# Adjacency products of a GRU layer from an fp32r high part and the rest: two one-pass matmuls in place of one two-pass fp32 matmul

## The chip, the cores and the metric

One core of a Trainium2 chip runs the whole program. The metric is the time of one execution in device microseconds (us), the median of several. Every experimental kernel was timed in three rounds beside the kernel before, on the same chip. The experiments ran in five batches on five chips, where before took 6768 to 6788 us (medians), so kernels of different batches are best compared by their ratios to before.

## The reference

64 graphs of 256 nodes with 256 features pass through three attention layers and one GRU layer. Every layer starts with a layer norm and a relu, and adds its result to x. The change is in the GRU layer. Cut to what matters:

```python
# layers 0, 1, 2: graph attention: softmax over neighbours, then attention @ features
# layer 3:
h = relu(layernorm(x))
A = (adj != 0).astype(float32)
for i in range(3):
    aggr = einsum('bst,bsd->btd', A, h @ weight[i])   # A is 0 or 1
    h = gru_cell(aggr, h, w_ih, w_hh, b_ih, b_hh)
return x + h
```

## The kernel before

Two graphs (a pair, 512 nodes) are worked on at a time, so there are 32 pairs. While TensorE does the attention layers of one pair, the GRU work of the pair before it is put between them. Each of the three GRU steps has a block of adjacency products ("block 1, 2, 3"), which read node features `hn` by rows and the adjacency `am`. All of it is fp32:

```python
def norm_t(xt, want_rows=False):
    ...                                            # layer norm to xn, transposed to ht
    hn = work.tile([P, C, D], F32, name="hn")
    nc.gpsimd.tensor_scalar(hn, xn, 0.0, None, op0=OP.max)          # L203
    return ht, hn
...
for h in range(H):                                 # layer 1, four heads
    for t in range(T):                             # five edge types
        nc.tensor.matmul(                          # L335: HT = 20 rows only
            ps, lhsT=ident[:HT, r : r + 1].to_broadcast([HT, P]), rhs=ed, ...)
...
for i in range(L):                                 # the GRU's three steps
    for dc in range(DC):
        for b in range(2):
            for sc in range(2):
                nc.tensor.matmul(                  # L415: a block is 8 of these
                    ps[:, b * N : (b + 1) * N],
                    lhsT=hn[:, 2 * b + sc, dc * P : (dc + 1) * P],
                    rhs=am[:, 2 * b + sc, :], start=(sc == 0), stop=(sc == 1))
        nc.scalar.copy(ag[:, dc, :], ps)
    ...                                            # gate products (L431), activations
    for b in range(2):                             # the new state, transposed to rows (L469)
        ...
        elif b == 0:
            nc.vector.tensor_copy(dst, ps)         # L480
        else:
            nc.scalar.copy(dst, ps)
```

## Time and profile before

| | before |
|---|---|
| time, median of 3 (range) | 6774.84 us (6770.32 to 6777.54) |
| TensorE busy | 5559.1 us, 82% of the span |
| VectorE (DVE), ScalarE (ACT), GpSimd (POOL) busy | 54%, 41%, 22% |
| mean granted TensorE clock | 0.829 |
| period of one pair (mean of 30) | 206.15 us |
| of it at half clock | 67.5 us |

TensorE is the bound: in most of a pair it works without a gap. But its granted clock is 1.00 or 0.50, never anything else (full and half clock below; "warm" is full clock), and in a third of the pair, 67.5 of 206.15 us, it is 0.50. A product of L431 follows the one before it after 0.43 us at full clock and 0.85 us at half, and "busy" counts that longer time.

Every stretch at one clock, but for the one that the end of the trace cuts off, is a whole multiple of 3.413 us long (at half clock mostly 3.41, 6.83 or 10.24 us), and all changes of the clock lie on one grid of that step, to within 0.01 us. One such step is called a window here. In before a half-clock stretch of 3.41 us starts at 3013.40, 1.06 us behind B's idle of 2.42 us, and one of 10.24 us starts at 3047.53, among eight 20-row products (L335), with TensorE 100% busy on both sides of the change (windows 3043.00:3047.53 and 3047.54:3057.77).

For all kernels I cut the pair into nine stretches at the same instructions: S1 (block 1 to the scores of layer 0's last head), A (to that head's first transpose, a wait for its softmax), S2 (to layer 0's last attention product), B (to the first transpose of layer 1's norm, a wait), S3 (layer 1, the long one), C (to the norm of layer 2, a wait), S4, D (the softmax of layer 2, a wait), S5.

### The profile page before, as it was taken

How to read it: one execution, taken by the hardware profiler on the slowest of the kernel's cores; microseconds unless marked ns; L12 is line 12 of the kernel's file. 1: busy time of each engine (PE TensorE's matmuls, PEld its weight loads, DVE VectorE, ACT ScalarE, POOL GpSimd, SP SyncE). 2: the span in 40 equal slices, each digit the busy share in tenths (PEclk: the TensorE clock that was granted, in tenths of full speed). 3: DMA queues.
4: the chain of work that ended last, by engine and by line, in shares of the span. 5: the costliest groups of instructions: out<-in, count | busy, mean ns of one | idle time of the engine just before them, and what ended most of it. 6: DMA issues, size and time to landing. Idle time of an engine off the chain costs nothing.

```text
span 6767.9 us, 53845 instructions
## 1 busy us (share of the span) xinstructions
PE 5559.1 (82%) x18480; PEld 3152.6 (47%) x18480; DVE 3627.6 (54%) x5756; ACT 2765.8 (41%) x6925; POOL 1512.0 (22%) x967
## 2 busy tenths in 40 slices
PE   5688988888978889888889788788878897888887
PEld 3444544444544445444445444445444454444453
DVE  4555555555555555555555555555555555555553
ACT  2344443344433444434444334444334443344442
POOL 1222122221122221222211222212222112222111
PEclk7788888888888878888788888888888888887888
DMA  1000000000000000000000000000000000000000
GB/s 54 0 10 10 4 10 7 10 10 10 4 7 10 10 10 4 10 7 10 10 10 4 7 10 10 10 10 4 7 10 10 10 4 7 10 10 7 4 1 6
DMA packets 55361, 59.15 MB, mean 9 GB/s; under 512 B 3120, under 2 KB 54192, under 8 KB 55088
## 3 DMA queue, kind: packets, MB, share of 16 engines
q1 hardware_dynamic: 54080, 53.88, 2.7%
q8 instruction: 146, 2.39, 0.2%
q10 hardware_dynamic: 1008, 1.84, 0.1%
q14 instruction: 127, 1.04, 0.1%
HBM read 38.93 MB, written 16.78 MB: 8 GB/s over the span
## 4 chain that ended last, share of the span: by engine, by line
PE 70%; DVE 16%; POOL 10%; ACT 2%; issue 1%; DMA 0%; DVEq 0%; POOLq 0%; SPq 0%; ACTq 0%
PE bank_psb L431 29%; PE bank_psa L335 11%; PE bank_psa L260 8%; PE bank_psa L245 5%; PE bank_psb L415 5%; PE bank_psa L211 4%; PE bank_psa L222 3%; DVE st L181 2%; DVE u L230 2%; DVE nm L232 2%; PE bank_psa L196 2%; POOL rstd L185 2%; POOL var L367 1%; POOL hn L203 1%; POOL en L305 1%; ACT u L235 1%
## 5 line engine op out<-in xcount | busy, mean ns | idle before, releaser
L431 PE MATMUL bank_psb<-ag,wc 128*128 128x512 f32 x2304 | 1263.5, 667 | 0.0
L431 PE MATMUL bank_psb<-ht,whh 128*128 128x512 f32 x2304 | 1217.6, 647 | 0.0
L457 POOL TENSOR_TENSOR d<-ht,n 128x512 f32<-128x512 f32 x192 | 254.6, 1326 | 3774.4 <-ACT n L451 3774.4
L342 ACT ACTIVATE e<-bank_psa,wh 128x256 f32<-128x256 f32 x2560 | 981.0, 478 | 282.8 <-PE bank_psa L335 270.9
L346 DVE COPY_PREDICATED u<-masks,e 128x1024 f32<-128x1024 uint8 x640 | 832.7, 1301 | 361.7 <-ACT e L342 359.7
L335 PE MATMUL bank_psa<-ed,ident 20*128 20x512 f32 x1280 | 775.0, 744 | 0.7 <-ACT ed L326 0.7
L235 ACT ACTIVATE u<-u,nm 128x256 f32<-128x256 f32 x1152 | 570.2, 497 | 429.3 <-DVE nm L232 420.5
L196 PE MATMUL bank_psa<-ident,xn 128*128 128x128 f32 x1024 | 202.8, 346 | 659.3 <-DVE xn L188 639.7
L431 PEld LDWEIGHTS bank_psb<-ag,wc 128*128 128x128 f32 x2304 | 477.5, 216 | 562.1 <-issue 547.5
L260 PEld LDWEIGHTS bank_psa<-wh,pt 128*128 128x128 f32 x4608 | 647.4, 205 | 146.5 <-issue 79.8
L431 PEld LDWEIGHTS bank_psb<-ht,whh 128*128 128x128 f32 x2304 | 439.7, 202 | 580.6 <-issue 566.6
L260 PE MATMUL bank_psa<-wh,pt 128*128 128x64 f32 (+1 forms) x4608 | 691.1, 302 | 0.1
L245 PE MATMUL bank_psa<-ident,u 128*128 128x128 f32 x2304 | 443.8, 313 | 264.8 <-ACT u L235 264.4
L245 PEld LDWEIGHTS bank_psa<-ident,u 128*128 128x128 f32 x2304 | 310.8, 158 | 568.0 <-ACT u L235 499.7
L199 ACT ACTIVATE ht<-bank_psa 128x512 f32<-128x512 f32 x256 | 146.0, 596 | 847.0 <-PE bank_psa L196 840.6
L196 PEld LDWEIGHTS bank_psa<-ident,xn 128*128 128x128 f32 x1024 | 148.7, 168 | 726.2 <-issue 596.1
L415 PE MATMUL bank_psb<-am,hn 128*128 128x256 f32 x1536 | 452.2, 447 | 7.5 <-POOL hn L203 2.6
L335 PEld LDWEIGHTS bank_psa<-ed,ident 20*128 20x128 f32 x1280 | 256.4, 215 | 333.3 <-issue 259.3
L415 PEld LDWEIGHTS bank_psb<-am,hn 128*128 128x128 f32 x1536 | 332.3, 228 | 115.0 <-issue 33.2
L269 DVE TENSOR_TENSOR o<-bank_psa,rs 128x256 f32<-128x256 f32 x256 | 108.7, 425 | 497.0 <-PE bank_psa L260 491.2
L469 PE MATMUL bank_psb<-ident,ht 128*128 128x128 f32 x768 | 166.8, 345 | 239.6 <-DVE ht L459 239.6
L455 ACT ACTIVATE z<-bank_psb,bg 128x512 f32<-128x512 f32 x192 | 131.8, 687 | 566.9 <-PE bank_psb L431 566.9
(89 smaller groups left out, 6671.2 us busy)
## 6 DMA issues: line engine op xcount, KB each, us to landing
xt<-in_x_dram SPq DMA_DIRECT2D x32, 512.0 KB, 4.9
at<-in_adj_dram SPq DMA_DIRECT2D x32, 512.0 KB, 3.8
out_dram<-hn SPq DMA_DIRECT2D x32, 512.0 KB, 3.2
whh<-in_L_gnn_w_hh_dram SPq DMA_DIRECT2D x1, 768.0 KB, 8.8
w<-in_L_gnn_weight_dram SPq DMA_DIRECT2D x3, 256.0 KB, 4.4
wih<-in_L_gnn_w_ih_dram SPq DMA_DIRECT2D x1, 768.0 KB, 6.6
a1b<-in_L_gnn_a_src_dram ACTq DMA_DIRECT2D x1, 640.0 KB, 7.2
a1b<-in_L_gnn_a_dst_dram ACTq DMA_DIRECT2D x1, 640.0 KB, 9.7
```

The costliest lines, as they stand in the source:

```text
L196: nc.tensor.transpose(ps[:, c * P : (c + 1) * P], xn[:, c, dc * P : (dc + 1) * P], ident)
L211: nc.tensor.matmul(ps[:, :m], lhsT=ht[:, dc, c * P : (c + 1) * P], rhs=we[:, dc, :m], start=(dc == 0), stop=(dc == DC - 1),)
L222: nc.tensor.matmul(ps, lhsT=wd[:, dc, h : h + 1].to_broadcast([P, P]), rhs=ht[:, dc, :], start=(dc == 0), stop=(dc == DC - 1),)
L235: nc.scalar.activation(u[:, c, :], u[:, c, :], AF.Exp, bias=nm[:, c : c + 1], accum_out=sm[:, c : c + 1])
L245: nc.tensor.transpose(ps[:, jc * N + ic * P : jc * N + (ic + 1) * P], u[:, 2 * b + ic, jc * P : (jc + 1) * P], ident,)
L260: nc.tensor.matmul(ps, lhsT=pt[:, b, jc, ic * P : (ic + 1) * P], rhs=wh[:, 2 * b + jc, f0:f1], start=(jc == 0), stop=(jc == 1),)
L335: nc.tensor.matmul(ps, lhsT=ident[:HT, r : r + 1].to_broadcast([HT, P]), rhs=ed, start=True, stop=True,)
L342: nc.scalar.activation(e[:, c, :], ps[:, b * N : (b + 1) * N], AF.Identity, bias=wh[:, c, D + r : D + r + 1],)
L346: nc.vector.copy_predicated(u, masks[:, t], e)
L415: nc.tensor.matmul(ps[:, b * N : (b + 1) * N], lhsT=hn[:, 2 * b + sc, dc * P : (dc + 1) * P], rhs=am[:, 2 * b + sc, :], start=(sc == 0), s ...
L431: nc.tensor.matmul(ps, lhsT=w[:, dc, g * P : (g + 1) * P], rhs=v[:, dc, :], start=(k == 0), stop=(k == n - 1),)
L457: nc.gpsimd.tensor_tensor(d, ht[:, j, :], n, op=OP.subtract)
```

## The change

The products of the blocks are to become cheaper. Before, each is two hardware matmuls ("two-pass" below: 768 in the source, 1536 in the profile, 0.22 us each at full clock). The adjacency is 0 or 1. An fp32 feature is split into a high part, written as fp32r, and the rest. Each part then takes one hardware matmul ("one-pass": still 1536 matmuls, for twice as many products), and both parts are summed in the same fp32 tile `ps` (`start` and `stop` in the diff). The order of TensorE's instructions is left to the scheduler, so it changes too. Docstrings and comments also went.

```diff
-        hn = work.tile([P, C, D], F32, name="hn")
-        nc.gpsimd.tensor_scalar(hn, xn, 0.0, None, op0=OP.max)
+        hn = work.tile([P, 2, C, D], F32R, name="hn")
+        nc.gpsimd.tensor_scalar(hn[:, 0], xn, 0.0, None, op0=OP.max)
+        nc.vector.scalar_tensor_tensor(
+            hn[:, 1], xn, 0.0, hn[:, 0].bitcast(F32), op0=OP.max, op1=OP.subtract
+        )
@@ gru
-        am = work.tile([P, C, N], F32, name="am", bufs=1)
+        am = work.tile([P, C, N], F32R, name="am", bufs=1)
@@
-                        nc.tensor.matmul(
-                            ps[:, b * N : (b + 1) * N],
-                            lhsT=hn[:, 2 * b + sc, dc * P : (dc + 1) * P],
-                            rhs=am[:, 2 * b + sc, :],
-                            start=(sc == 0), stop=(sc == 1),
-                        )
+                        for part in range(2):
+                            nc.tensor.matmul(
+                                ps[:, b * N : (b + 1) * N],
+                                lhsT=hn[:, part, 2 * b + sc, dc * P : (dc + 1) * P],
+                                rhs=am[:, 2 * b + sc, :],
+                                start=(sc + part == 0), stop=(sc + part == 2),
+                            )
@@
-            hn = work.tile([P, C, D], F32, name="hn")
+            if last:
+                res = work.tile([P, C, D], F32, name="res", bufs=1)
+            else:
+                hn = work.tile([P, 2, C, D], F32R, name="hn")
@@
-                elif b == 0:
-                    nc.vector.tensor_copy(dst, ps)
                 else:
-                    nc.scalar.copy(dst, ps)
+                    nc.scalar.copy(pair(hn[:, 0]), ps)
+                    nc.vector.tensor_sub(pair(hn[:, 1]), ps, pair(hn[:, 0]).bitcast(F32))
```

More of the change, by code (lines that the diff above doesn't have):

```diff
@@ L9 @@
 F32 = mybir.dt.float32
+F32R = mybir.dt.float32r
 I32 = mybir.dt.int32
@@ L473, in gru, with pair @@
                         )
-                dst = hn[:, 2 * b : 2 * b + 2, :].rearrange("p c d -> p (c d)")
+                def pair(t):
+                    return t[:, 2 * b : 2 * b + 2, :].rearrange("p c d -> p (c d)")
                 if last:
-                    nc.vector.tensor_add(
-                        dst, xt[:, 2 * b : 2 * b + 2, :].rearrange("p c d -> p (c d)"), ps
-                    )
-                elif b == 0:
-                    nc.vector.tensor_copy(dst, ps)
-                else:
-                    nc.scalar.copy(dst, ps)
+                    nc.vector.tensor_add(pair(res), pair(xt), ps)
+                else:
+                    nc.scalar.copy(pair(hn[:, 0]), ps)
+                    nc.vector.tensor_sub(pair(hn[:, 1]), ps, pair(hn[:, 0]).bitcast(F32))
             yield
-        nc.sync.dma_start(out_v[:, p * C : (p + 1) * C, :], hn)
+        nc.sync.dma_start(out_v[:, p * C : (p + 1) * C, :], res)
         yield
```

## The prediction

> **What bounds the kernel now.** I read the page first (busy shares, chain, groups), then the timeline of TensorE over one pair of graphs, then windows with the granted clock.
>
> ```profile
> span 6767.9 us, 53845 instructions
> ...
> PE 5559.1 (82%) x18480; PEld 3152.6 (47%) x18480; DVE 3627.6 (54%) x5756; ACT 2765.8 (41%) x6925; POOL 1512.0 (22%) x967
> ...
> PE 70%; DVE 16%; POOL 10%; ACT 2%; issue 1%; DMA 0%; DVEq 0%; POOLq 0%; SPq 0%; ACTq 0%
> ...
> L415 PE MATMUL bank_psb<-am,hn 128*128 128x256 f32 x1536 | 452.2, 447 | 7.5 <-POOL hn L203 2.6 <-DVE hn L480 0.9
> ```
>
> TensorE is the bound, but not everywhere: 70% of the chain that ended last is its own work, 26% is DVE and POOL work for which it stands idle. The products that the change touches (L415) take 452 of 5559 us. Each source matmul is two hardware ones here (768 in the source, 1536 in the row).
>
> The timeline of TensorE shows the period of one pair, 206.1 us on average (first L415 of pair 1 at 279.2 us, of pair 31 at 6463.7, 30 periods). It has four stretches in which TensorE waits for a chain of other engines, whatever else it has to do: A, the softmax of layer 0's last head; B, the layer norm after layer 0; C, the norms after layer 1; D, the softmax of layer 2. B looks so:
>
> ```profile
> 3000.69 1.00 PE L260 MATMUL bank_psa<-wh,pt 128*128 128x64 f32 x8
> 3001.53 3.24 PE L415 MATMUL bank_psb<-am,hn 128*128 128x256 f32 x14
> 3004.60 1.88 PE L431 MATMUL bank_psb<-ht,whh 128*128 128x512 f32 x4
> 3006.32 1.88 PE L431 MATMUL bank_psb<-ag,wc 128*128 128x512 f32 x4
> 3008.04 1.88 PE L431 MATMUL bank_psb<-ht,whh 128*128 128x512 f32 x4
> 3012.34 2.04 PE L196 MATMUL bank_psa<-ident,xn 128*128 128x128 f32 x8 [2.42 <-DVE xn L188]
> ```
>
> The last attention product of layer 0 (L260) ends at 3001.53; the norm that follows from it reaches TensorE at 3012.34, 10.8 us later. In between lie 14 of the 16 L415 matmuls, and TensorE idles 2.42 us at the end. This is a wait for DVE, so a shorter L415 only lengthens the idle. Starts divided by counts: an L415 matmul takes 0.22 us (3.07/14), an L431 0.43 us (1.72/4).
>
> The windows show the clock:
>
> ```profile
> core 0: us, PE busy (x) PEld busy (x) DVE busy (x) ACT busy (x) POOL busy (x), PEclk, DMA share, GB/s
> 3050.50:3057.00 6.50, 6.50 (x8) 2.08 (x7) 3.85 (x3) 3.02 (x8) 0.00 (x0) 0.50 0.00 0
> 3071.50:3074.80 3.30, 3.30 (x10) 2.55 (x9) 2.60 (x2) 3.30 (x9) 0.00 (x0) 0.50 0.00 0
> 3076.40:3083.30 6.90, 6.90 (x17) 3.08 (x17) 5.38 (x5) 3.66 (x9) 0.00 (x0) 1.00 0.34 76
> 2958.30:3163.90 205.60, 171.22 (x577) 96.09 (x577) 112.62 (x179) 86.14 (x216) 47.24 (x30) 0.84 0.03 8
> ```
>
> TensorE runs at half or full clock, and can be at 0.50 while 100% busy. Over one pair the mean is 0.84, so about a third of the time is at half speed. The half-speed stretches follow the L335 matmuls, which have 20 rows only, and the idle times.
>
> [...]
>
> **The change, part by part.**
> Removed: 1536 two-pass L415 matmuls of 0.22 us, warm. Added: 1536 one-pass ones (768 x 2 parts). I take each at 0.11 us[...]. That is 16 x 0.11 = 1.76 us less in each of the three blocks of a pair, warm. In the third block, which lies partly at half clock (its matmuls take 5.8 to 6.5 us), up to about 3 less. Were all of it on the path: 32 x (1.76 + 1.76 + 3) = 209 us, 3.1%. That is the ceiling.
>
> Added on DVE: per pair one 128x1024 subtract (1.22 us, as L230) and four 128x512 from PSUM (0.68) against two copies (0.67): +2.6 us; ACT two more copies of 0.58. Neither is near full, so this counts as latency only. After the transposes TensorE must now wait for an ACT copy and then a DVE subtract, where two copies ran beside each other.
>
> Order matters more. The compiled orders of both kernels have the same 72 gate products (0.86 us each, two matmuls) per pair, but the scheduler spreads them differently. Before, 12 lie inside the waits A, B, C, where they are free or nearly so (4, 6 and 2; one more, after B's wait, is alike in both). After, 7 (2, 5, 0). So 5 gate products move onto TensorE-bound stretches: 2 between D and A, 3 between B and C.
>
> Block 1 (after layer 3's norm):
>
> ```profile
> 3161.03 2.78 POOL L203 TENSOR_SCALAR hn<-xn 128x1024 f32<-128x1024 f32 x1 [1.58 <-DVE xn L188]
> 3163.82 1.66 DVE L294 SCALAR_TENSOR_TENSOR u<-bank_psa,wh,cap 128x256 f32<-128x256 f32 x4 [2.96 <-PE bank_psa L222]
> 3163.86 3.72 PE L415 MATMUL bank_psb<-am,hn 128*128 128x256 f32 x16
> ```
>
> POOL's hn is ready at 3163.81, just as L415 starts. The low part needs one more DVE pass of 1.22 us, so TensorE stalls some 1.2 us of the 1.76 saved: 0.6 is won. The pass also stands ahead of L294, which starts 1.25 us later; the two gate products moved forward cover that. This stretch: -0.6 + 2 x 0.86 = +1.1 us.
> Up to the end of layer 0's last attention product: one L415 and five transposes moved behind it: -1.0 us.
> Block 2: inside B: 0. Its idle grows to about 2.9 us.
> Block 3 (layer 1, TensorE-bound): the transposes come late, behind the softmax; the second half's high part is copied by ACT only after four exponentials. I estimate 2 us of stalls, of which before shows half already. Net of that -2.7 us with its half clock, plus three gate products at mixed clock, +2.6 to +3.1: about +0.2 us.
> Sum: +0.3 us a pair.
>
> Clock: idle before A's end grows from 1.31 to about 3 us (3.4 of gate products became 1.7). B's 2.42 us made a half-speed window of 3.41 us; A's 1.31 did not. So A may now do so, which costs up to 1.7 us. In block 3's half-speed window there is now half the L421 work beside two 20-row matmuls, so a second such window is likely in some pairs. I put +0.8 us on both. Total +1.1 us a pair, x 32 = +35 us: 6775 + 35 = 6810 us.
>
> **The rivals.**
> First, "the saving goes through": TensorE is 82% busy, so 209 us less work gives 3% less, 6570 us. For it: the 70% of the chain. Against it: block 2 is inside a wait, block 1 loses most to the new DVE pass, and freed time in A to C is not refilled.
> Second, "the clock takes it": more idle and thinner work mean more half-speed windows; two more a pair cost 3.4 us, 32 x 3.4 = 109 us, 6880 to 6920 us. For it: periods before come as 204.8, 205.6 and 207.4 us, in step with 3.41 us windows, so small shifts may jump by a window.
> Third, "the new chain binds": copy then subtract in the ACT and DVE queues delays transposes and softmax of the next head, +2 us a pair, 6840 to 6870 us. For it: the queue order at block 3. Against it: ACT 41% and DVE 54% busy.
> Fourth, one-pass matmuls that do not run at 0.11 us (weight loads not overlapped): at 0.2 us nothing is saved, and the time is near 6900 us.
>
> **Range and chances.** The first rival is damped by the arithmetic above, and half of it (3 us a pair) gives 6680. The second and third together give 6930. So 6810, range 6700 to 6930. Faster by over 2% (below 6639) needs nearly all the ceiling on the path, 0.08; slower by over 2% (above 6910) needs two extra half-speed windows or slow one-pass matmuls, 0.12; the rest 0.80.
>
> **What will show it.** In the changed profile the L421 group should have 1536 matmuls, about 0.11 us apart when warm, and TensorE's busy time should fall by 150 to 230 us at a span that hardly moves. The idle at L197 for DVE xn, and at L250 for ACT u, should grow; new idle should stand at L421 for DVE hn (1.2 us in block 1, more in block 2). DVE should write hn 160 times (five a pair). The clock should be at or a little below 0.83. I am wrong if the period drops below 203 us: then the moved gate products or block 3's stalls cost less than I take them for, or half-speed windows vanish.

## The result, and the profile after

The kernel after takes 6932.65 us (median of 4, 6931.14 to 6933.39) against 6776.19 us (median of 4) in the same rounds: ratio 1.0234, interval 1.0220 to 1.0249, **slower by over 2%**. A ratio here is the mean time of one kernel's fast runs over that of the other's of the same rounds, so not quite the ratio of the medians quoted. The prediction was 6810 us, with 6700 to 6930 as its range; the measured time lies just outside. All outputs are right.

The page of the kernel after (span; busy time by engine; the chain that ended last; the group of the changed products, with busy time, mean ns of one, and idle time before them):

```profile
span 6931.6 us, 53910 instructions
...
PE 5604.3 (81%) x18480; PEld 3201.7 (46%) x18480; DVE 3766.8 (54%) x5852; ACT 2800.4 (40%) x6989; POOL 1534.2 (22%) x967
...
PE 70%; DVE 17%; POOL 8%; ACT 2%; issue 2%; DMA 0%; DVEq 0%; SPq 0%; ACTq 0%; POOLq 0%
...
L421 PE MATMUL bank_psb<-am,hn 128*128 128x256 f32 x1536 | 364.2, 391 | 34.9 <-DVE hn L206 27.1
```

The changed products did get shorter (452.2 to 364.2 us, though many now run at half clock). TensorE's busy time nevertheless rose, from 5559.1 to 5604.3 us. No work was added on TensorE, so the time of the same instructions rose: that is the clock, 0.794 on the mean after 0.829.

The waits of TensorE (who waited for whom; us in total, times, longest), before:

```profile
PE bank_psa L196 <- DVE xn L188: 639.7, 66, 24.2
PE bank_psa L245 <- ACT u L235: 264.4, 145, 6.6
PE bank_psb L469 <- DVE ht L459: 239.6, 65, 4.6
```

and after:

```profile
PE bank_psa L197 <- DVE xn L189: 704.7, 66, 24.2
PE bank_psa L250 <- ACT u L240: 312.9, 72, 6.6
PE bank_psb L478 <- DVE ht L465: 216.8, 65, 5.4
PE bank_psb L421 <- DVE hn L206: 27.1, 31, 0.9
```

The two old waits grew by 65 and 49 us, the third shrank by 23, and the new wait at L421 is 27 us. That is 118 us in all; with the 45 us more of busy time (5559.1 to 5604.3) it makes the 163 us by which the span grew (163.7).

The timeline of TensorE after (start, length, then idle before it and its releaser), at block 1 and from stretch A to the end of B:

```profile
3031.87 0.38 PE L421 MATMUL bank_psb<-am,hn 128*128 128x256 f32 x1
3033.13 2.06 PE L421 MATMUL bank_psb<-am,hn 128*128 128x256 f32 x15 [0.88 <-DVE hn L206]
...
3069.04 0.38 PE L478 MATMUL bank_psb<-ident,ht 128*128 128x128 f32 x2
3072.93 0.45 PE L250 MATMUL bank_psa<-ident,u 128*128 128x128 f32 x1 [3.50 <-ACT u L240]
...
3079.89 3.81 PE L421 MATMUL bank_psb<-am,hn 128*128 128x256 f32 x16
...
3089.44 1.41 PE L197 MATMUL bank_psa<-ident,xn 128*128 128x128 f32 x8 [1.46 <-DVE xn L189]
```

Block 1 is as foreseen: a stall of 0.88 us, then 15 products in 1.90 us (3033.13 to 3035.03), 0.127 us each. Stretch A ends with 3.50 us of idle, and block 2 takes 3.64 us for 16 (to 3083.53), 0.23 each: it lies at half clock.

The windows after (length, then busy time and instructions of PE, PEld, DVE, ACT and POOL, then the clock):

```profile
3144.67:3154.91 10.24, 10.24 (x19) 4.43 (x18) 7.10 (x6) 7.79 (x21) 0.00 (x0) 0.50 0.17 51
3072.99:3083.23 10.24, 10.21 (x44) 8.89 (x45) 2.54 (x5) 4.21 (x11) 3.81 (x2) 0.50 0.00 0
3031.87:3243.50 211.63, 173.50 (x577) 99.09 (x577) 117.13 (x182) 87.22 (x218) 48.03 (x30) 0.80 0.03 8
```

The second line is the half-clock time that starts 0.06 us after A's idle has ended; the prediction's pair has none there. The first line lies in head 3 of layer 1, around block 3, with TensorE 100% busy: 10.24 us at half clock, where the prediction's pair has 3.41 (its line at 3071.50 shows 3.30 of them). What TensorE does there before:

```profile
3067.23 3.69 PE L335 MATMUL bank_psa<-ed,ident 20*128 20x512 f32 x8
3070.86 4.54 PE L415 MATMUL bank_psb<-am,hn 128*128 128x256 f32 x12
3075.33 1.12 PE L335 MATMUL bank_psa<-ed,ident 20*128 20x512 f32 x2
```

and after:

```profile
3142.70 5.27 PE L340 MATMUL bank_psa<-ed,ident 20*128 20x512 f32 x8
3147.89 2.07 PE L421 MATMUL bank_psb<-am,hn 128*128 128x256 f32 x8
3149.90 2.07 PE L340 MATMUL bank_psa<-ed,ident 20*128 20x512 f32 x2
```

Between two lots of products with 20 rows stood 4.5 us of products with 128 rows; now 2.0 us stand there, and half clock covers them all and runs on.

By stretch (mean of 30 pairs, worked out from the traces; us, and in brackets how much of it at half clock; e2b, e3b and e4b are experiments below):

```
        before          after           e2b             e3b             e4b
S1      32.23 (0)       33.69 (0)       34.09 (0)       33.05 (0)       33.69 (0)
A        6.90 (0)        7.37 (0.01)     7.37 (0.62)     6.90 (0)        7.37 (0)
S2       4.15 (0)        5.65 (5.58)     5.65 (5.65)     5.69 (4.17)     3.69 (0)
B       10.82 (0)       10.86 (4.65)    10.86 (3.97)    10.87 (6.07)    10.82 (0.38)
S3      98.01 (36.18)   99.91 (40.85)   93.55 (21.16)  100.32 (40.62)  101.93 (43.99)
C       25.17 (20.63)   25.70 (22.59)   25.71 (23.42)   25.17 (17.76)   25.70 (22.63)
S4+D+S5 28.87 (10.65)   28.45 (11.55)   27.91 (10.72)   29.51 (12.97)   28.42 (11.51)
pair   206.15 (67.5)   211.63 (85.2)   205.15 (65.5)   211.50 (81.6)   211.63 (78.5)
```

In B and C TensorE waits for other engines, and half clock costs next to nothing there: B takes 10.82 us with none of it, 10.86 with 4.65 us (before, after). In S2 and S3 I take it to cost half its length, as with the products of L431 (0.85 us for 0.43). That is an estimate, and for S2 a high one: e4b has 5.58 us less of it there than after, and S2 is 1.96 us shorter, not 2.8. Taking that half off gives what these stretches would take at full clock, waits included: S1 + A + S2 + S3 is 123.20 us before and 123.40 after. So that hardly changed, and (5.58 + 40.85 - 36.18) / 2 = 5.1 of the 5.48 us that a pair got longer are, by that estimate, half clock in S2 and S3.

The same can be counted over the whole pair, with TensorE's busy time (as at full clock), its idle time, and what half clock adds to the busy time (taken as half of the busy time at half clock) kept apart (us a pair, worked out from the same traces; e8 and e9 are before and after with 128 rows in place of 20):

```
              before   after    e2b      e8       e9
work          148.4    143.0    148.3    146.2    142.5
idle           34.3     38.1     37.0     36.7     40.8
half clock     23.4     30.5     19.8     11.6     11.3
pair          206.15   211.63   205.15   194.55   194.56
```

So the saving was there, 5.4 us a pair, and 3.9 us of it became idle time; half clock then took 7.0: 5.0 of them in S1 to S3, where they lengthen the pair, and 2.3 in B, which stayed at 10.8 us. (Before and e8 have the same products with the same columns and differ by 2.2 us in work, so read no difference finer than that.)

### The profile page after: what moved, and what is told of

It is laid out like the page before. It is cut to its first block, busy times and chain, and to the rows that moved or that the text cites. A ratio compares the mean times of both kernels' runs of the same rounds, so it can differ in the third digit from the quotient of the medians.

```text
span 6931.6 us, 53910 instructions
## 1 busy us (share of the span) xinstructions
PE 5604.3 (81%) x18480; PEld 3201.7 (46%) x18480; DVE 3766.8 (54%) x5852; ACT 2800.4 (40%) x6989; POOL 1534.2 (22%) x967
## 4 chain that ended last, share of the span: by engine, by line
PE 70%; DVE 17%; POOL 8%; ACT 2%; issue 2%; DMA 0%; DVEq 0%; SPq 0%; ACTq 0%; POOLq 0%
PE bank_psb L437 30%; PE bank_psa L340 12%; PE bank_psa L265 9%; PE bank_psa L250 6%; PE bank_psa L216 4%; PE bank_psa L227 3%; PE bank_psb L421 3%; DVE st L182 2%; DVE u L235 2%; POOL rstd L186 1%; POOL var L372 1%; PE bank_psa L197 1%; POOL hn L205 1%; POOL en L310 1%; DVE ht L465 1%
## 5 line engine op out<-in xcount | busy, mean ns | idle before, releaser
L437 PE MATMUL bank_psb<-ht,whh 128*128 128x512 f32 x2304 | 1326.2, 696 | 0.0
L437 PE MATMUL bank_psb<-ag,wc 128*128 128x512 f32 x2304 | 1162.2, 620 | 0.0
L340 PE MATMUL bank_psa<-ed,ident 20*128 20x512 f32 x1280 | 855.5, 816 | 0.7 <-ACT ed L331 0.7
L197 PE MATMUL bank_psa<-ident,xn 128*128 128x128 f32 x1024 | 181.2, 322 | 724.1 <-DVE xn L189 704.7
L265 PEld LDWEIGHTS bank_psa<-wh,pt 128*128 128x128 f32 x4608 | 695.7, 220 | 142.9 <-issue 65.1
L437 PEld LDWEIGHTS bank_psb<-ht,whh 128*128 128x128 f32 x2304 | 476.4, 220 | 614.3 <-issue 606.4
L265 PE MATMUL bank_psa<-wh,pt 128*128 128x64 f32 (+1 forms) x4608 | 742.0, 318 | 0.1
L250 PE MATMUL bank_psa<-ident,u 128*128 128x128 f32 x2304 | 470.2, 331 | 313.6 <-ACT u L240 312.9
L257 DVE COPY pt<-bank_psa 128x512 f32<-128x512 f32 x288 | 199.1, 691 | 400.0 <-PE bank_psa L250 400.0
L421 PE MATMUL bank_psb<-am,hn 128*128 128x256 f32 x1536 | 364.2, 391 | 34.9 <-DVE hn L206 27.1
L448 ACT ACTIVATE r<-bank_psb,bg 128x512 f32<-128x512 f32 x192 | 131.3, 684 | 607.1 <-PE bank_psb L437 607.1
L421 PEld LDWEIGHTS bank_psb<-am,hn 128*128 128x128 f32 x1536 | 297.4, 275 | 148.8 <-issue 47.7
```

Of the source, the lines that this page charges most:

```text
L197: nc.tensor.transpose(ps[:, c * P : (c + 1) * P], xn[:, c, dc * P : (dc + 1) * P], ident)
L250: nc.tensor.transpose(ps[:, jc * N + ic * P : jc * N + (ic + 1) * P], u[:, 2 * b + ic, jc * P : (jc + 1) * P], ident,)
L265: nc.tensor.matmul(ps, lhsT=pt[:, b, jc, ic * P : (ic + 1) * P], rhs=wh[:, 2 * b + jc, f0:f1], start=(jc == 0), stop=(jc == 1),)
L340: nc.tensor.matmul(ps, lhsT=ident[:HT, r : r + 1].to_broadcast([HT, P]), rhs=ed, start=True, stop=True,)
L421: nc.tensor.matmul(ps[:, b * N : (b + 1) * N], lhsT=hn[:, part, 2 * b + sc, dc * P : (dc + 1) * P], rhs=am[:, 2 * b + sc, :], start=(sc + ...
L437: nc.tensor.matmul(ps, lhsT=w[:, dc, g * P : (g + 1) * P], rhs=v[:, dc, :], start=(k == 0), stop=(k == n - 1),)
```

## The experiments

Two questions: is it the new order of TensorE's instructions or the one-pass products themselves; and is the clock the cause, or only what goes with a new chain of waits (copy, then subtract)?

### Order and operations apart

To hold an order, every matmul and transpose is recorded where it is made, and at the end each GRU instruction is tied behind and ahead of its neighbours by edges of the class NoSync. (The profiles of these kernels show the lines of the helpers, L173 to L184.)

```diff
+    for p in range(NP - 1):
+        last = None
+        for k, m in ORDER:     # which GRU instruction, how many of the attention's stand before it
+            g, m = made["gru"][p * ng + k], na * (p + 1) + m
+            if last is not None:
+                behind(g, last)
+            last = g
+            for q in made["att"][m - 8 : m]:
+                behind(g, q)
+            for q in made["att"][m : m + 8]:
+                behind(q, g)
```

The first table held only counts, not which instruction stands where, so a transpose that must wait for the GRU's state (L469) came before gate products that need not. Four runs have this flaw. e2 is the old operations in the order of after; e3 the new operations with the gate products where before has them; e4 is after with three products that nobody reads in A's idle; e7 is before with 128-row products (edit below).

> The kernel before (fp32 products, its own copies), with TensorE's instructions held in the changed kernel's order (two fewer gate products in the wait for the last softmax of layer 0, three more in layer 1). Theory 'order and clock': the idle before that softmax grows from 1.31 us to about 3 us, the half-clock window that follows in the changed kernel appears here too, and the gate products that left the waits add 4 us: 6 to 8 us a pair more, 6950 to 7020 us, clock near 0.79. Theory 'new chain' (the extra copy and subtract make the changed kernel slower, order does not matter): within 1% of 6775 us.

Measured: 6828.03 us, ratio 1.0088 [1.0071, 1.0104].

> The changed kernel, with the gate products put where the kernel before has them (four in the wait for the last softmax of layer 0, six in the wait for the norm after it, two after layer 1), all else as in the changed kernel's order. Theory 'order and clock': idle before that softmax falls from 3.5 to about 1.8 us, no half-clock stretch after it, S1 1.7 us and layer 1 2.6 us shorter: about 205 us a pair, 6700 to 6790 us, clock 0.82 or more. Theory 'new chain': stays at 6880 to 6935 us.

Measured: 6842.20 us, ratio 1.0108 [1.0093, 1.0123].

> The changed kernel in its own order, with three idle fp32 products of 128x512 (2.6 us, read by nobody) for TensorE in the wait for the last softmax of layer 0. Theory 'clock': TensorE idles 0.9 us there instead of 3.5, the 10.24 us at half clock that follow do not come, the 2.7 us that the transposes and attention products lost there come back: about 209 us a pair, 6830 to 6870 us. Theory 'the idle costs only itself': 6930 us, or more by what the filler delays.

Measured: 7032.32 us, ratio 1.0389 [1.0374, 1.0405].

> The kernel before in its own order, with the 20-row products of layer 1 (L335) made over 128 rows, the added ones zero: the same columns, so the same time at a given clock. If the clock gate looks at how much of the array works: most of layer 1's 36 us at half clock a pair vanish, up to 18 us a pair: 6250 to 6600 us, clock 0.88 or more. If it looks at something else (idle time alone, or the values, which are zero): 6775 us within 1%.

Measured: 6367.21 us, ratio 0.9407 [0.9393, 0.9421], clock 0.883.

The waits of e2 show the flaw (before, this wait came 65 times and cost 239.6 us):

```profile
PE bank_psb L178 <- DVE ht L472: 324.0, 96, 3.6
```

In e4 the filling products queued behind such a transpose and stretch A grew to 11.70 us. So e2, e3 and e4 decide nothing by themselves; in e7 the effect is far larger than the flaw. The table then named each instruction, and the runs were repeated.

> As e2, but with each transpose of the GRU's state in its own place too (e2 held only the counts, and TensorE waited for a state in the wait for the last softmax). fp32 products and the copies of before, TensorE in the changed kernel's order. Theory 'order and clock': an idle of over 3 us before that softmax, a half-clock stretch after it, S1 and layer 1 longer by the gate products that left the waits: 4 to 8 us a pair, 6900 to 7020 us, clock 0.79 to 0.80. Theory 'new chain': within 1% of 6770 us. e2's 6828 would say that order is a third of it.

Measured: 6731.44 us, ratio 0.9946 [0.9932, 0.9961]. The old operations in the new order are a little *faster* than before. Its column in the table has S2 at half clock just as after has (5.65), so A's idle and what follows it come with the order. Yet the pair takes 205.15 us, because S3 has only 21.16 us at half clock.

> As e3, with the GRU's transposes in the changed kernel's own places. One-pass products, gate products in the waits as before the change. Theory 'order and clock': idle before the last softmax of layer 0 1.8 us, no half-clock stretch after it: about 205 us a pair, 6700 to 6790 us, clock at least 0.82. Theory 'new chain': 6880 to 6935 us. e3 gave 6842 with the misplaced transposes.

Measured: 6928.40 us, ratio 1.0233 [1.0216, 1.0250]. The new operations with the old places of the gate products are as slow as after. (Its transposes stand as in after; A's gate products as in before.)

Both results lie where the theory "new chain" had them, so a chain of waits has to be told from the clock in another way. The waits of e2b, which has the copies of before and the order of after:

```profile
PE bank_psa L178 <- DVE xn L201: 669.1, 64, 24.2
PE bank_psa L178 <- ACT u L248: 313.0, 73, 6.6
PE bank_psb L178 <- DVE ht L472: 215.0, 65, 3.6
PE bank_psb L173 <- DVE hn L493: 26.6, 33, 0.9
```

These are nearly those of after (704.7, 312.9, 216.8 and 27.1), without its chain: most of the longer waits came with the order. What after has more than e2b is half clock (85.2 us a pair for 65.5).

Together: with two-pass products a pair takes 206.15 and 205.15 us in the two orders, with one-pass products 211.50 and 211.63. The order is worth 1 us at most; **the operations cost 5.4 to 6.5 us a pair**. What the stretches would take at full clock, by the estimate of half the length, ranks them otherwise: S1 + A + S2 + S3 is then 123.2 us before, 126.9 in e2b, 123.6 in e3b and 123.4 after. The new order costs the two-pass products 3.7 us (gate products have left the waits, as predicted), and in that order one-pass products save 3.5. The kernel that by this would be slowest at full clock is the fastest of the four.

### A's idle filled

```diff
+            if h == H - 1:      # layer 0's last head; nobody reads it
+                fl = bank(psa)
+                for _ in range(3):
+                    nc.tensor.matmul(fl, lhsT=ident, rhs=whh[:, 0, :512], start=True, stop=True)
             pt, rs = softmax_t(u, 0.2)
```

> As e4, with the filler behind transposes that need not wait: every engine's order is that of the changed kernel, three fp32 products of 128x512 that nobody reads are added in the wait. Theory 'clock': idle there falls from 3.5 us to about 0.9, no half-clock stretch follows, S2 falls from 5.65 to about 3.1 us and the rest of the pair is as it was: 209 us a pair, 6840 to 6870 us, clock 0.82. Theory 'the idle costs only itself': 6930 us within 0.3%.

Measured: 6927.64 us, ratio 1.0232 [1.0217, 1.0247]. Its timeline (L322 are the fillers, L181 transposes, L176 other products):

```profile
3066.62 2.74 PE L322 MATMUL bank_psa<-whh,ident 128*128 128x512 f32 x6
3070.28 0.33 PE L181 MATMUL bank_psa<-ident,u 128*128 128x128 f32 x1 [0.92 <-ACT u L255]
...
3084.80 1.44 PE L181 MATMUL bank_psa<-ident,xn 128*128 128x128 f32 x5 [2.81 <-DVE xn L204]
```

The local effect is as the theory has it: with 0.92 us of idle in place of 3.50, S2 stays at full clock and falls from 5.65 to 3.69 us. So A's idle does set off half clock in after, as the prediction feared: 5.58 us of it behind 3.50 us of idle, none behind 0.92. (It need not be 3.50 us: e3b has A's idle of before, 1.31 us, and 0.45 more just behind it, and still 4.17 us of half clock in S2, where before has none. What makes the difference was not taken apart.) But the pair takes 211.63 us as before the edit, to the hundredth. In after, 4.65 us of half clock lie inside the wait B, where they are free; with the filler only 0.38 do, and S3 has 3.1 us more of it and is 2.0 us longer. The gain was taken back.

### Twenty rows made 128

The 20-row products are given 128 rows: rows 20 to 127 of both operands are zero, so the result is the same and the number of columns too. At full clock the time of one is as good as the same: 0.429 us from one 20-row product to the next in before (median), 0.43 with 128 rows in e8 (ten in 4.29 us, 2868.55 to 2872.84).

```diff
+    ed = consts.tile([P, S], F32, name="ed")     # once, at the start
+    nc.gpsimd.memset(ed, 0.0)
-        ed = work.tile([HT, S], F32, name="ed", bufs=1)
-        nc.scalar.copy(ed, ps[:HT, :])
+        nc.scalar.copy(ed[:HT, :], ps[:HT, :])
-                    ps, lhsT=ident[:HT, r : r + 1].to_broadcast([HT, P]), rhs=ed,
+                    ps, lhsT=ident[:, r : r + 1].to_broadcast([P, P]), rhs=ed,
```

e8 is this on before and e9 this on after, each in the order of its own. e10 is e9 with the high part of layer 3's norm made by VectorE in place of GpSimd (`nc.gpsimd.tensor_scalar(hn[:, 0]` becomes `nc.vector.tensor_scalar(hn[:, 0]`), which takes the stall at block 1 away. e11 is e2b with 128 rows, e12 is e4b with 128 rows.

> The kernel before with its own free order (identical to before on every engine, checked), the 20-row products made over 128 rows, the added ones zero. e7 held the order and misplaced transposes, which cost it an idle and a half-clock stretch of 3.4 us before the attention product; without that about 2 us a pair less than e7: 6300 to 6340 us, half-clock time in layer 1 at or below e7's 8.2 us a pair. Had e7's gain come from its order, not from the rows: 6700 us or more.

Measured: 6399.83 us, ratio 0.9453 [0.9439, 0.9467], clock 0.879. Stretch S3 of one pair of before, then of e8:

```profile
3012.34:3111.25 98.91, 95.47 (x269) 47.41 (x269) 54.92 (x63) 54.45 (x139) 10.07 (x6) 0.81 0.03 6
2858.11:2944.98 86.87, 81.01 (x269) 45.41 (x269) 53.48 (x63) 54.08 (x139) 10.34 (x6) 0.92 0.03 7
```

TensorE has the same 269 instructions in both; half clock in S3 fell from 36.2 to 13.7 us, the pair to 194.55 us. So busy time alone doesn't tell the clock here: the same products with 108 more rows, of zeros, have 22.5 us less of half clock in S3, and TensorE was 100% busy through 10.24 us at clock 0.50 in after.

> The changed kernel with the 20-row products over 128 rows, order on every engine as in the changed kernel; to be set against e8 (6400 us, 194.55 us a pair). Theory 'the change moves little work, the 20-row products' half-clock time takes the rest': work at full clock +0.8 us a pair, half clock in S2 after the 3.5 us idle +2.8 at most: 195.3 to 198.2 us a pair, 6420 to 6520 us. Theory 'the change itself costs 2.3%': 6545 us. Theory 'the saving goes through once the clock is clean': below 6330 us.

Measured: 6398.90 us, ratio 0.9453 [0.9438, 0.9467], clock 0.870. With 128 rows the kernels before and after take the same time. All else of the change (the order, the stalls, the longer chain) is still in e9; only the 2.3% are gone. That the two agree to the hundredth of a us a pair is no measure of the rest of the change, though: e8, e9, e10 and e12 all take 194.55 us, 57.00 windows (below), though e10 has 0.8 us less in S1 than e9 and e12 1.95 us less in S2, so a difference of that size could be hidden either way. What the table above shows is that half clock costs the two the same (11.6 and 11.3 us). Its timeline at the place shown above:

```profile
2910.59 3.65 PE L341 MATMUL bank_psa<-ed,ident 128*128 128x512 f32 x8
2913.68 1.51 PE L422 MATMUL bank_psb<-am,hn 128*128 128x256 f32 x8
2915.03 1.02 PE L341 MATMUL bank_psa<-ed,ident 128*128 128x512 f32 x2
```

The same 18 products as after, from 2910.59 to 2915.89, take 5.3 us; after, they took 9.2 (3142.70 to 3151.90).

> e9 with the first layer's high part made by DVE instead of POOL (DVE idles 2.96 us there in the profile before), TensorE's and ACT's order unchanged. Theory: POOL's 2.78 us and then DVE's 1.22 make the stall of the low part and delay the softmax; with 0.7 and 1.22 us on DVE from 3160.9 on both end before TensorE comes to them: no idle for DVE hn at the products, S1 1.2 us shorter, A 0.4 us shorter: 1.2 to 1.7 us a pair below e9, 40 to 55 us. Rival: the stall is in another stretch's shadow: within 10 us of e9.

Measured: 6390.83 us, ratio 0.9441 [0.9425, 0.9456]. The wait at block 1 is gone from the list of waits, and S1 is 0.8 us shorter; but the pair stays at 194.55 us, and the time is only 0.1% less.

> fp32 products and copies of before, TensorE in the changed kernel's order, 128 rows. e2b had this order with 20 rows and was faster than before (6731 us) since its layer 1 happened to have 21 us at half clock for 36. Theory: without the 20-row products the order's cost shows: S1 +1.9, S3 +3.1 (three gate products), S2 +1.5 at half clock, A +0.5: 6 to 7 us a pair above e8, 6580 to 6620 us. Rival 'order is harmless': within 1% of e8's 6400 us.

Measured: 6506.86 us, ratio 0.9612 [0.9597, 0.9626]. At 128 rows, the old operations in the new order are slower than the new ones by 1.7%.

> e9 with the filler of e4b (three fp32 products in the wait for layer 0's last softmax). e4b took S2 from 5.65 to 3.69 us but its layer 1 then had 3.1 us more at half clock and the period stayed 62 windows. Theory 'layer 1's 20-row products took it back': with 128 rows the 2 us stay won: 1.5 to 2.5 us a pair below e9, 45 to 80 us. Rival 'the period is a whole number of 3.41 us windows whatever one does': equal to e9 within 0.3%, or one window (110 us) off.

Measured: 6392.93 us, ratio 0.9445 [0.9431, 0.9459]. S2 is at full clock and 1.95 us shorter, S3 1.6 us longer than in e9; the pair is 194.55 us again.

### Idle products on a stretch at full clock

The runs so far leave open whether after was only unlucky in how its pair falls on the windows of 3.41 us. So idle products of 0.86 us each were put among the gate products of layer 0's second head (in S1, bound by TensorE, at full clock), 1, 2 and 4 to before (e13), 2 and 4 to after (e14), each in its own order. The edit is that of e4b with `h == 1` and another number. e15 is after without the stall in block 1 (the edit of e10 alone).

> The kernel before, TensorE's order held as it is, plus one fp32 product of 128x512 (0.86 us at full clock, read by nobody) a pair, among the gate products of layer 0, where TensorE never waits and the clock is full. Theory 'the clock's windows set the period': it settles on a whole number of 3.413 us windows, 60 (204.8 us a pair, about 6728 us) or 61 (208.2 us, 6834 us). Theory 'work adds up': +0.86 us a pair, 207.0 us, 6797 us.

Measured: 6825.19 us, ratio 1.0054 [1.0039, 1.0069].

> The same with two such products, 1.72 us. Windows: 61 (6834 us) or 62 (211.6 us, 6940 us). Adding up: 207.9 us a pair, 6823 us, which is near 61 windows, so this one alone tells little; the three together do.

Measured: 6758.91 us, ratio 0.9956 [0.9941, 0.9971].

> The same with four, 3.43 us, one window's worth. Windows: 61 (6834 us) or 62 (6940 us). Adding up: 209.6 us a pair, 6876 us.

Measured: 6875.79 us, ratio 1.0130 [1.0111, 1.0147].

> The changed kernel (20-row products) with the first layer's high part on DVE: TensorE's order as in the changed kernel, S1 0.8 us shorter as e10 showed against e9. Work adds up: 211.6 - 0.8 = 210.8 us a pair, 6907 us. Windows: 62 as before that (6932 us within 10) or 61 (208.2 us, 6826 us) or fewer.

Measured: 6926.44 us, ratio 1.0204 [1.0188, 1.0219] (before was at 6787.92 in these rounds, above its usual 6770).

> The kernel after in its own order, with two idle 512-column products (0.86 us each, 1.72 us together, nobody reads them) among the gate products of layer 0's second head, a stretch that is bound by TensorE and ran at full clock throughout. 'Work adds up': the period rises by 1.72 us a pair, 31 pairs, +53 us, 6981 us. 'The period settles on whole 3.413 us windows and after sits on 62 with slack': either no change at all (62.00 windows, 6928 us) or a jump to 63 (215.0 us, 7035 us) or to a mean between; a rise of 1.72 would be 62.5, only possible as an alternation of 62 and 63. 'After has bad luck with its phase': it could fall to 61 (6820 us). Its half-clock time in the long stretch of layer 1 should move by several us against the 40.9 of after.

Measured: 7013.27 us, ratio 1.0350 [1.0331, 1.0369].

> As the run with two, with four idle products (3.43 us, one whole window). 'Work adds up': +106 us, 7034 us. 'Whole windows': 3.43 us is one window and 0.02, so if the pattern of the clock is carried along unchanged the period is 63.0 windows, 7035 us, and the half-clock time of the long stretch stays at 41; if the later stretch can absorb it, 62.00 windows again. Not told apart by this run alone: the first two give the same; it is here beside the run with two, where they differ.

Measured: 7128.36 us (one run of four at 7087.38), ratio 1.0499 [1.0462, 1.0536].

The periods of a pair in windows (3.4133 us, the step measured in the traces of before and after) are:

```
before 60.40   +1: 61.00   +2: 60.30   +4: 61.44      e2b 60.10
after  62.00   -0.8 us (e15): 62.00   +2: 62.80   +4: 63.87      e3b 61.96   e4b 62.00
128 rows: e8 57.00   e9 57.00   e10 57.00   e11 58.00   e12 57.00   e7 56.70
```

Single pairs of e14 with two products take 211.6 or 215.0 us, 62 or 63 windows, and nothing between; before alternates 205.6 and 207.4, 121 windows for two. What makes a period settle on such a number, no run isolates. Small edits, at any rate, don't add up: 0.86 us more cost before 2.05, 1.72 more saved 0.34; 0.8 us less gave after nothing.

But luck is not the whole. Over these fillings and orders the two kinds of kernel keep apart in the mean half clock in head 3 of layer 1 (between the ends of the attention products of heads 2 and 3, mean of 30 pairs; the pair in brackets):

```
two-pass   before 4.78 (206.15)  +1 6.83 (208.20)  +2 4.44 (205.81)  +4 4.89 (209.71)  e2b 3.64 (205.15)
one-pass   after 10.24 (211.63)  +2 10.35 (214.36)  +4 10.35 (218.00)  e15 10.24 (211.63)  e3b 10.24 (211.50)  e4b 11.95 (211.63)
128 rows   e8 2.49   e9 0.00   e10 0.00   e11 0.00   e12 0.00
```

Even the flawed ones keep to it on the mean (e2 5.12; e3 10.54, e4 13.43), though single pairs overlap (14 of e3's 30 have 6.8 us, one of e2b's has 10.2). In after it is 10.2 us in each of 30 pairs; before, 3.4 or 6.8. The half clock of the whole pair keeps apart as well, the flawed ones included: 62 to 72 us with two-pass products, 78 to 91 with one-pass ones; with 128 rows it is 42 to 51 for both kinds. The periods do not all: the flawed e2 and e3 take 208.33 and 208.77 us, hardly apart, and e3 is below before with four products (209.71). So the loss is shown for the two orders compared above; its size hangs on the order. With the same filling, after is 8.6 (two products) and 8.3 us (four) above before.

## Why the prediction was wrong, point by point

**Products.** Right: 1536 of them, 0.127 us apart at full clock (predicted about 0.11, the author's estimate: half of the 0.22 before), 0.23 at half clock.

**Block 1.** Right: the stall is 0.88 us (predicted 1.2), VectorE's pass takes 1225 ns on the mean, S1 grew by 1.46 us (predicted 1.1).

**S2, B and S3 at full clock.** Right in the sum, by the estimate of half the length. A grew by 0.47 us, S2 fell by 1.29 (predicted 1.0; e4b, at full clock there, shows 0.46), S3 fell by 0.43 (predicted +0.2), B stayed at 10.8. The sum is +0.2 us, predicted +0.3. B's idle should grow to about 2.9 us: it is 2.81 in e4b; in after only 1.46, since its block 2 runs at half clock. The stalls foreseen in blocks 2 and 3 did not come: the 31 waits for hn at L421 are all block 1's (0.9 us at most), and TensorE's idle in S3 is 3.1 us, before 3.4.

**A's idle.** Right: 3.50 us (predicted about 3), and it did make half clock, as e4b shows by filling it.

**The clock.** This is the step that failed, and by its size. It stood in the prediction twice: A "may now do so, which costs up to 1.7 us", and "In block 3's half-speed window there is now half the L421 work beside two 20-row matmuls, so a second such window is likely in some pairs. I put +0.8 us on both." Measured, the first is 5.58 us of half clock in S2, in every pair, worth 2.8 us by the estimate of half its length (S2 in e4b: 1.96 less); the second is 10.24 us in place of 4.78 in head 3, worth 2.7 by the same estimate, in every pair. The rest of S3 gave back a part (head 1 and its lead-in 6.8 us less at half clock, head 2 and head 4 6.0 more), so that both stretches together cost 5.1 us, where the prediction put 0.8. 32 x 5.1 = 163 us; the loss was 156.

**Busy time of TensorE** was to fall by 150 to 230 us and rose by 45. The work did fall, by 5.4 us a pair or some 170 us in all; but the check left out that half clock lengthens the other products as well (L431: 0.85 us for 0.43).

**The rivals.** The second, "two more a pair", 6880 to 6920 us, was the true one in kind, and it was kept out of the expected value because I gave it the weight of a chance. In size it was short: S2 and S3 have 10.25 us more at half clock, three windows, and 6932.65 us lies above it. The third, the new chain, falls: e2b has nearly the waits of after without that chain, and the one stall that is the chain's own, at block 1, is 0.88 us a pair. Removing it is worth 0.1% (e10 against e9; e15, 6926.44 us, against the 6932.65 of after), but the periods stayed at 57.00 and 62.00 windows, so what it might be worth by itself is not shown. The fourth, slow one-pass products, falls with the 0.127 us. So does a reading that the new order is to blame: e2b has the order and is faster than before.

**The range.** Its upper end comes from a wrong sum: "The second and third together give 6930", but 109 and 64 us on 6775 are 6948. The right sum would have taken the result in, but with a cost of the new chain that did not come.

What is shown: the loss is half clock; it needs both the one-pass products and the 20-row products (take either away and it goes: e2b, e9); and without A's long idle S2 has none (e4b). What is argued only: that in head 3 it is the shortness of the full-row work between the 20-row lots that matters. The timelines of before and after fit that, but e2b speaks against it as the whole reason: 6 two-pass products stand between the same two lots there, 1.30 us at full clock (in e11), where after's 8 take 1.35 (in e9; 0.4 of it is a pause behind the first), and yet head 3 of e2b has only 3.64 us of half clock. What else sets the two apart was not measured. After with block 3's products doubled for nothing would tell; it was not run. Also open is why a kernel settles on one number of windows and not on the next: A's half clock was removed in e4b and the pair stayed at 62.00.

**A version that beats both** came out of it: e10 (6390.83 us), the changed kernel with 128-row products, 5.6% below before. e7 is faster still (6367.21 us, 5.9% below) with the old operations and an order that was a mistake; with periods that stayed at 57.00 or 62.00 windows under the small edits of e10, e12, e4b and e15, I would not read that as a merit of its order.

## What to carry to other kernels

Before pricing a saving on TensorE, read the granted clock around the saved instructions, before and after: here the products got 88 us cheaper (452.2 to 364.2) while half clock grew from 67.5 to 85.2 us a pair. Where matmuls that use few rows stand in number, try them with all rows, the added ones zero: here, with 20 rows made 128, the time of one at full clock stayed at 0.43 us and the kernel got 5.5% faster. In a periodic kernel read a change of a few us by the half-clock time of each stretch and by the period (here 57.00, 58.00, 61.00 or 62.00 times 3.413 us in nine of the runs), and try several fillings before a small gain or loss is believed.
